# A written issue order, stores on ScalarE's queue and a rewritten 3x3 in a two-layer bottleneck kernel

## The chip, the cores and the metric

The kernel runs on one core of one Trainium2 chip. The metric is the device time of one execution in microseconds (us), as the median of several executions. Their spread is under 0.7% for every kernel. Ratios are computed from the mean time of one kernel's runs over the mean time of the other's in the same rounds on the same chip; they are therefore not quite the ratios of the medians that are quoted beside them. An interval behind a ratio is a 95% interval.

## The reference

Sixteen images of 1024 x 32 x 32 in float32 pass through two residual blocks. The first has a local attention in its middle, the second a 3x3 convolution. Cut to what matters:

```python
def _L0_conv_ref(x, ...):                       # attention block
    residual = x
    h = relu(bn(conv1x1(x, w_conv1)))           # 1024 -> 256
    h = self_att(h, ...)                        # q, k, v: 256 -> 256; 3x3 window, 32 heads of 8, softmax over 9
    h = bn(conv1x1(h, w_conv3))                 # 256 -> 1024
    return relu(h + residual)

def _L1_conv_ref(x, ...):                       # plain block
    out = relu(_bn(_conv(x, w1)))               # 1024 -> 256
    out = relu(_bn(_conv(out, w2, padding=1)))  # 3x3, 256 -> 256
    out = _bn(_conv(out, w3))                   # 256 -> 1024
    return relu(out + x)
```

## The kernel before

TensorE's work for one image is a chain of seven stages: the *attention expansion* (256 -> 1024, tiles `a,w`), the *reduction* of the second block (`r,u`), the *first convolution* of the image two further on (`x,w`), the *3x3* by a Winograd scheme (`v,U`), the *projection* of q, k, v for that later image (`h,wqkv`), its position offsets (`q,pos`), and the *last expansion* (`h,u`). VectorE does the attention of the later image beside these.

An expansion makes its 1024 channels in eight *chunks* of 128. Each chunk has its residual put into PSUM, the memory in which TensorE adds up its products, by ScalarE ahead of the products ("seed" below). ScalarE also evicts the result, and the store follows:

```python
def expand_conv(b, wt, src, shift):
    ahead = []
    def seed(o):
        if o < NC:
            ps = psum.tile([P, HW], F32, tag="ps", name="ps")
            nc.scalar.activation(ps, xr[b, o], AF.Identity)        # residual into PSUM
            ahead.append(ps)
    seed(0)
    seed(1)
    for o in range(NC):
        ps = ahead.pop(0)
        ...                                                        # 8 matmuls onto ps
        nc.scalar.activation(xr[b, o], ps, RELU, bias=shift(o), scale=1.0)
        seed(o + 2)
        yield o

def expand_last(b):
    behind = 2
    for o in expand_conv(b, take("u3", b), hidden_one.pop(b), ...):
        nc.sync.dma_start(out[b, o * P : (o + 1) * P, :], xr.pop((b, o)))   # store
        if o >= behind:
            load_residual(b + 1, o - behind)                                # nc.sync, same buffers
        yield o
    ...
```

The attention works in another layout than the projection writes. So q (`qc<-q`), k (`bnk<-kp`), v (`bnv<-vh`), the offsets (`pc<-po`) and the attention's output (`a<-acc`) are moved by small DMA copies, all issued by SyncE, 36 for an image. The exponential of the softmax is one instruction of ScalarE, between VectorE's logits and VectorE's weighted sum:

```python
        nc.vector.tensor_tensor(e, e, mx..., ALU.subtract)
        nc.scalar.activation(e, e, AF.Exp)
        yield 4.7
```

In this kernel a scheduler chooses the order in which each engine issues; the order of writing is only a wish.

## Time and profile before

| | before |
|---|---|
| median of the three executions before the change was run | 3201.35 us (3199.76 to 3202.84) |
| TensorE busy | 82% of 3198.2 us, mean granted clock 0.908 |
| idle of TensorE before the attention expansion | 442.5 us |
| start to start of that expansion, mean of 13 images | 193.9 us |
| first such start, image 0, image 14 | 216.5, 206.8, 126.6 us |

The last two rows are differences of starts in TensorE's timeline. The kernel has 16 images; 13 of them are alike, the first and the last two are not. So a total is the first start, plus the image 0, plus 13 alike, plus image 14, plus what is left after the start of image 15. The prediction below shows the lines that it rests on.

### The profile page before, as it was taken

How to read it: one execution, taken by the hardware profiler on the slowest of the kernel's cores; microseconds unless marked ns; L12 is line 12 of the kernel's file. 1: busy time of each engine (PE TensorE's matmuls, PEld its weight loads, DVE VectorE, ACT ScalarE, POOL GpSimd, SP SyncE). 2: the span in 40 equal slices, each digit the busy share in tenths (PEclk: the TensorE clock that was granted, in tenths of full speed). 3: DMA queues.
4: the chain of work that ended last, by engine and by line, in shares of the span. 5: the costliest groups of instructions: out<-in, count | busy, mean ns of one | idle time of the engine just before them, and what ended most of it. 6: DMA issues, size and time to landing. Idle time of an engine off the chain costs nothing. (4 is left out here: it accounts for less than half of the span.)

```text
span 3198.2 us, 19613 instructions
## 1 busy us (share of the span) xinstructions
PE 2632.5 (82%) x7072; PEld 1347.0 (42%) x7072; DVE 1959.8 (61%) x1771; ACT 893.6 (28%) x851; POOL 5.0 (0%) x11
## 2 busy tenths in 40 slices
PE   6688579697895969969698796978969699696898
PEld 2335235253352524525244352533525245252545
DVE  2859765855649466485755659566495664757613
ACT  2031322313233132421323223132321324223143
POOL 0000000000000000000000000000000000000000
PEclk9789889798897989989899897989989899798999
DMA  7862726649175491835838276491744828357242
GB/s 226 239 127 76 136 77 166 162 126 198 56 158 151 134 199 60 153 141 151 176 98 179 76 168 160 128 200 58 154 154 141 186 65 169 120 128 173 78 146 92
DMA packets 192783, 446.75 MB, mean 140 GB/s; under 512 B 18096, under 2 KB 124592, under 8 KB 180144
## 3 DMA queue, kind: packets, MB, share of 16 engines
q1 hardware_dynamic: 189696, 434.71, 54.3%
q10 hardware_dynamic: 2992, 10.80, 1.0%
q8 instruction: 57, 0.93, 0.1%
q14 instruction: 38, 0.31, 0.0%
HBM read 285.52 MB, written 73.40 MB: 112 GB/s over the span
## 5 line engine op out<-in xcount | busy, mean ns | idle before, releaser
L289 PE MATMUL ps<-a,w 128*128 128x512 f32 x1024 | 476.3, 628 | 442.5 <-ACT ps L280 442.5
L407 DVE TENSOR_TENSOR prod<-qc,bnk 128x2048 f32<-128x2048 f32 x144 | 323.9, 2287 | 423.4 <-DMA bnk<-kp 252.7
L289 PEld LDWEIGHTS ps<-a,w 128*128 128x128 f32 x1024 | 206.0, 203 | 712.6 <-ACT ps L280 454.7
L260 PE MATMUL ps<-x,w 128*128 128x512 f32 x1024 | 448.7, 598 | 38.2 <-DMA x<-in_x_dram 26.7
L536 PE MATMUL ps<-v,U 128*128 128x256 f32 x2048 | 451.2, 383 | 19.4 <-issue 19.4
L289 PE MATMUL ps<-h,u 128*128 128x512 f32 x1024 | 447.1, 597 | 9.9 <-ACT h L580 9.9
L260 PE MATMUL ps<-r,u 128*128 128x512 f32 x1024 | 442.1, 592 | 0.0
L536 PEld LDWEIGHTS ps<-v,U 128*128 128x128 f32 x2048 | 393.4, 192 | 81.9 <-issue 28.0
L510 DVE TENSOR_TENSOR tv<-vh 128x1088 f32<-128x1088 f32 x64 | 82.4, 1287 | 460.1 <-ACT vh L497 459.5
L340 PE MATMUL ps<-h,wqkv 128*128 128x512 f32 x768 | 339.5, 598 | 3.3 <-ACT kp L350 3.3
L260 PEld LDWEIGHTS ps<-x,w 128*128 128x128 f32 x1024 | 196.3, 192 | 283.9 <-issue 256.4
L289 PEld LDWEIGHTS ps<-h,u 128*128 128x128 f32 x1024 | 195.9, 192 | 257.9 <-issue 245.5
L260 PEld LDWEIGHTS ps<-r,u 128*128 128x128 f32 x1024 | 194.6, 190 | 244.9 <-issue 244.9
L465 DVE TENSOR_TENSOR acc<-acc,term 128x2048 f32<-128x2048 f32 x128 | 291.7, 2279 | 0.6
L453 DVE TENSOR_TENSOR term<-e,bnv 128x2048 f32<-128x2048 f32 x128 | 289.9, 2284 | 0.0
L280 ACT ACTIVATE ps<-r 128x1024 f32<-128x1024 f32 x256 | 257.5, 1021 | 13.8 <-DVE m L558 3.8
L340 PEld LDWEIGHTS ps<-h,wqkv 128*128 128x128 f32 x768 | 145.6, 191 | 188.6 <-issue 179.7
L297 ACT ACTIVATE r<-ps,par 128x1024 f32<-128x1024 f32 x128 | 142.6, 1114 | 244.9 <-PE ps L289 184.8
L515 DVE TENSOR_TENSOR v<-tv 128x512 f32<-128x512 f32 x256 | 160.7, 688 | 75.9 <-DMA a<-acc 68.0
L297 ACT ACTIVATE r<-ps,bn_sh 128x1024 f32<-128x1024 f32 x128 | 142.5, 1113 | 203.4 <-PE ps L289 203.4
L410 DVE TENSOR_TENSOR prod<-prod 128x1024 f32<-128x1024 f32 x144 | 170.3, 1220 | 0.0
L435 ACT ACTIVATE e<-e 128x2304 f32<-128x2304 f32 x16 | 34.0, 2122 | 432.8 <-DVE e L434 432.8
(72 smaller groups left out, 1105.7 us busy)
## 6 DMA issues: line engine op xcount, KB each, us to landing
x<-in_x_dram SPq DMA_DIRECT2D x128, 512.0 KB, 3.7
r<-in_x_dram SPq DMA_DIRECT2D x128, 512.0 KB, 6.2
U<-uw SPq DMA_DIRECT2D x64, 1024.0 KB, 4.9
out_dram<-r SPq DMA_DIRECT2D x128, 512.0 KB, 7.2
bnk<-kp SPq DMA_DIRECT2D x128, 170.0 KB, 10.8
bnv<-vh SPq DMA_DIRECT2D x128, 170.0 KB, 10.2
w<-in_w1t_dram SPq DMA_DIRECT2D x16, 1024.0 KB, 7.1
qc<-q SPq DMA_DIRECT2D x128, 128.0 KB, 5.6
```

The lines of the kernel that those rows point to most:

```text
L260: nc.tensor.matmul(ps[n][:, halves(half)], wt[:, c, n * P : (n + 1) * P], src[:, halves(half)], start=(c == 0), stop=(c == NC - 1),)
L280: nc.scalar.activation(ps, xr[b, o], AF.Identity)
L289: nc.tensor.matmul(ps[:, halves(half)], wt[:, n, o * P : (o + 1) * P], src[:, n, halves(half)], start=False, stop=(n == NW - 1), skip_grou ...
L297: nc.scalar.activation(xr[b, o], ps, RELU, bias=shift(o), scale=1.0)
L340: nc.tensor.matmul(ps[:, halves(half)], wqkv[:, m, at : at + P], h[:, m, halves(half)], start=(m == 0), stop=(m == NW - 1),)
L407: nc.vector.tensor_tensor(by_row(t), by_row(qc), kc[:, :, i : i + JROWS, j : j + W], ALU.mult)
L410: nc.vector.tensor_add(t[:, 0:4], t[:, 0:4], t[:, 4:8])
L453: nc.vector.tensor_tensor(by_row(dst), rows(e[:, k, :]).unsqueeze(1).to_broadcast([P, HEAD_DIM, JROWS, W]), vc[:, :, i : i + JROWS, j : j ...
L465: nc.vector.tensor_add(acc, acc, t)
L510: nc.vector.tensor_tensor(t, vh[:, :, i0 : i0 + 2 * NT - 1 : 2, :], vh[:, :, i1 : i1 + 2 * NT - 1 : 2, :], op)
L515: nc.vector.tensor_tensor(v[:, j].rearrange("p n (r w) -> p n r w", w=NT), t[:, :, :, j0 : j0 + 2 * NT - 1 : 2], t[:, :, :, j1 : j1 + 2 * ...
L536: nc.tensor.matmul(ps[:, at, n * TILES : (n + 1) * TILES], u[:, m, j, n * P : (n + 1) * P], v[:, j, m, :], start=(m == 0 and n == 0), stop ...
```

## The change

Its intent: the order of writing becomes the order of issue on every engine, and the code is written in the order of time. The residual copies for the next expansion come at the end of the last one, so that the exponential can't stand before them; stores go to ScalarE's queue, where the eviction that they wait for has just been issued; k is projected before q; and the 3x3 keeps three of its products in one bank, with ScalarE reading the partial sum on the way, to relieve VectorE. Cut to its core:

```diff
+    ctx.enter_context(tc.manual_schedule())
 ...
+    class Expand:
+        def seed(self):
+            ps = psum.tile([P, HW], F32, tag="ps", name="ps")
+            nc.scalar.activation(ps, xr[self.b, len(self.ahead)], AF.Identity)
+            self.ahead.append(ps)
+        def chunks(self, wt, src, then):
+            for o in range(NC):
+                ...
+                (self.seed if o + 2 < NC else then)()      # `then` seeds the following expansion
+                nc.scalar.activation(xr[self.b, o], ps, RELU, bias=self.shift(o), scale=1.0)
 ...
+        yield from halo("bnk", 1, RELU, kp)                # k, then q, then v and the offsets
+        for n in range(NW):
+            norm(q[:, n, :], conv(0, n), "bnq", n, RELU)
 ...
+        def second(i):                                     # 3x3: on the bank that ScalarE has read
+            products(i, 2, 0, False)
+            both = small("m12")
+            nc.scalar.activation(both, sums[i][:, 0], AF.Identity)
+            diffs[i] = small("d")
+            nc.vector.scalar_tensor_tensor(diffs[i], firsts[i], 2.0, both, ALU.mult, ALU.subtract)
+        def last(i):
+            products(i, 0, 0, False)
+            more_weights()
+            ...                                            # sums on VectorE
             if i + 2 < NU:
                 early.append(next(forms))                  # the transform for product group i + 2
 ...
+        for o in last.chunks(take("u3", b), hidden_one.pop(b), following.seed if following else nothing):
+            nc.scalar.dma_start(out[b, o * P : (o + 1) * P, :], xr.pop((b, o)))
+            if o >= BEHIND:
+                load_residual(b + 1, o - BEHIND)
+            if o == 4 and following:
+                finish_attended(b + 1)
```

The rest of the diff (cut) puts the preparation of the weights beside the first convolution and places the steps of the attention by estimated time.

## The prediction

> **What bounds the kernel now.** I read the page's busy times first, then the groups, the waits, the timeline of one steady image, the granted clock by stretch, and last the waits of the DMA queue.
>
> ```profile
> PE 2632.5 (82%) x7072; PEld 1347.0 (42%) x7072; DVE 1959.8 (61%) x1771; ACT 893.6 (28%) x851; POOL 5.0 (0%) x11
> ...
> L289 PE MATMUL ps<-a,w 128*128 128x512 f32 x1024 | 476.3, 628 | 442.5 <-ACT ps L280 442.5
> L407 DVE TENSOR_TENSOR prod<-qc,bnk 128x2048 f32<-128x2048 f32 x144 | 323.9, 2287 | 423.4 <-DMA bnk<-kp 252.7
> ...
> L260 PE MATMUL ps<-r,u 128*128 128x512 f32 x1024 | 442.1, 592 | 0.0
> ```
>
> TensorE (PE) is the busiest engine, and of its 566 us of idle time 442.5 us stand before one line: the expansion of the attention block (L289, a,w), which waits for ScalarE's copy of the residual into PSUM (L280). The same matmuls elsewhere (L260, r,u) wait for nothing. The timeline of one image shows why:
>
> ```profile
> 1354.77 8.32 PE L289 MATMUL ps<-h,u 128*128 128x512 f32 x19
> 1394.04 29.13 PE L289 MATMUL ps<-a,w 128*128 128x512 f32 x64 [30.95 <-ACT ps L280]
> 1423.01 27.63 PE L260 MATMUL ps<-r,u 128*128 128x512 f32 x64
> 1450.47 27.63 PE L260 MATMUL ps<-x,w 128*128 128x512 f32 x64
> 1477.94 27.79 PE L536 MATMUL ps<-v,U 128*128 128x256 f32 x128
> 1505.57 13.90 PE L340 MATMUL ps<-h,wqkv 128*128 128x512 f32 x32
> ```
>
> ```profile
> 1363.18 1.11 ACT L297 ACTIVATE r<-ps,bn_sh 128x1024 f32<-128x1024 f32 x1 [2.38 <-PE ps L289]
> 1390.95 2.12 ACT L435 ACTIVATE e<-e 128x2304 f32<-128x2304 f32 x1 [26.65 <-DVE e L434]
> 1392.98 2.90 ACT L280 ACTIVATE ps<-r 128x1024 f32<-128x1024 f32 x3
> ```
>
> (Columns: start, us, engine, work, idle before it and releaser.) ScalarE stands 26.65 us at the exponential of the next image but one, because VectorE is still computing its logits; the residual copies that TensorE needs are queued behind it. Nothing real joins the two. TensorE loses 31 us per image so. The start of L289 (a,w) goes from 423.37 to 2943.65 in 13 images: 193.9 us each.
>
> **What the Trainium skill says.** (1) "Perfetto Trace Analysis", Per-engine timelines: ScalarE and VectorE are strict first-in-first-out. The trace agrees: the copies above start 0.1 us before the exponential's row ends, never ahead of it. (2) "TensorE: Matmul & The Clock Gate", HAM oscillation: an idle gap above some 3.4 us drops the array to half clock, regained after some microseconds of work. The trace agrees: the first block after each gap takes 29.1 to 30.8 us, the same block without a gap 27.63, and the granted clock is 1.00 from 1423 to 1556 us but 0.58 from 1556 to 1586. So a gap costs about 2.5 us more. (3) "DMA: Bandwidth & Descriptors", Issuing engines are not separate DMA queues: issue from another engine saves sequencer time only, all use the same 16 DMA engines. The trace of before has only start-up copies on ScalarE's queue.
>
> **The change, part by part.** The work of one steady image on TensorE, from the spacing of starts: four blocks of 27.47, the 3x3 27.63, q, k, v and the offsets 13.83 + 1.87 + 6.97: 160.2 us. Matmul counts stay. That is the floor.
>
> *Written order, residual copies before the eviction.* The first two copies for the next expansion now come at chunks 6 and 7 of the last one; the exponential is written after some 18 steps of 3.0 us, thus behind the attention expansion's last eviction. VectorE's logits take 9 x 4.3 + 12 = 51 us in the trace (interleaved); written in order, dependent instructions follow each other at 0.46 us where independent ones take 0.34 (rows of 0.42 us), so I take 9 x 4.75 + 9 = 52. They end some 62 us after the expansion begins, the exponential's turn comes at about 57 to 68. ScalarE hardly waits and TensorE does not: -30.9 and -2.7 us (clock) per image.
>
> *Sums of the 3x3.* Products of four matmuls take 27.63/16 = 1.73 us. Each second product accumulates on a bank that ScalarE must first have copied (0.60 us), with one product between: hidden. VectorE drops from 16 x 0.685 + 4 x 1.22 = 15.8 to 16 x 0.685 = 11.0 us, ScalarE gains 6 x 0.6. But the fourth transform now stands behind two additions that wait for ScalarE's copy of the second sum: 15.5 (products end) + 0.9 + 1.4 + 1.3 + 1.3 = 20.4 us after the 3x3 begins, needed at 19.0. **+1.5 us.**
>
> *k first, stores on ScalarE's queue.* Here I expect a new wait. The DMA queue's own waits in one image:
>
> ```profile
> SPq L390 <- DMA bnk<-kp: 4.0, 4, 1.1
> SPq L369 <- DMA bnk<-kp: 3.9, 4, 1.0
> SPq L595 <- DMA bnv<-vh: 3.4, 3, 1.2
> ```
>
> The stores (L595) do not read bnv, yet wait for it. In the trace's DMA rows the completion semaphores are eight, taken in turn, and each issue waits for the transfer eight before; at start-up the two queues share the same eight. So a store on ScalarE will wait for a copy issued by SyncE, and ScalarE with it, since nothing passes a waiting issue. In the new order, from the start of the projection (p): k 8 copies, q 4, a 8, q 4, v 4, offsets 4, v 4, one weight, then store 0, whose eighth predecessor is the second offsets copy. The DMA engines are full there (share 1.04 and 1.11 from 1512 to 1556 us). In before 28 such copies land in 37 us; I split it as 1.5 us for k and v, 1.0 for q and a, 1.25 for offsets. Up to that copy: 8 x 1.5 + 8 + 8 + 4 x 1.5 + 2.5 = 36.5 us, from p + 5: p + 41. The expansion begins at p + 22.7, so store 0 is held to 18.5 us into it, not 4.9. Copies for chunks 0 to 2 are made before it; chunk 3 (due at 10.3) starts at 18.5 + 0.4 + 1.0 = 20: **+9.7 us, and 2 us of clock.** The later stores follow at the pace of the copies, 1.5 us apart, ahead of TensorE.
>
> Steady image: 160.2 + 1.5 + 11.7 = 173.4; 13 images: 2254 us.
>
> *The ends.* Start-up: the weights' preparation is put beside and behind the first convolution (it ends at 40.6), which then keeps the projection's evictions until about 64 us; the exponential of image 0 is written after the third convolution (about 147 us), and its weighted sum of 44 us, copies and evictions follow: the first expansion at about 208 us (216.5 before). Image 0 has no convolution beside it, so image 1's attention still has 40 us to do in the projection, and copies and stores wait for it: 190 us (206.8 before). Image 14: 25 us of attention are put before the stores: 144 (126.6). Image 15: 124 (123). Tail 5.
>
> Sum: 208 + 190 + 2254 + 144 + 124 + 5 = **2925 us** with the store wait.
>
> **Rivals.** *A: the stores don't hold ScalarE* (other semaphores, or the copies land sooner). Then a steady image is 161.9 us, image 0 some 178, image 14 some 133: 2753 us. For it: the change chooses this queue on purpose, and k first moves its copies some 7 us earlier. Against: the three lines above. *B: the wait for the exponential only moves,* with VectorE too late for the new place. 101 us of attention in order, 15 of transforms and 11 of sums are 127 us of 160, and its present idle 28 us after the projection shrinks; against it. If VectorE came 10 us late per image: 130 us more, about 3050. *C: VectorE in order bounds the 3x3:* if the third transform is late too, some 4 us more per image, 50 us.
>
> **Range and chances.** I give the store wait 65%, A 35%: 0.65 x 2925 + 0.35 x 2753 = 2865; I put 2870. The range takes A's sum less 15 as its low end, 2740, and the store wait with C, 2970, as its high end. Faster by over 2% means under 3137, which only B and more would miss: 0.98.
>
> **What would show it.** Right: the wait of L289 (a,w) for L280 falls from 442.5 us to under 60; the 3x3 shows a gap of 1 to 2 us before its 12th product; the expansion after the 3x3 shows one gap of 7 to 12 us before its fourth chunk, at L280, while ScalarE's queue waits for the offsets copies (pc). If that gap is missing A holds. Wrong: ScalarE idle for VectorE at the exponential with TensorE idle beside it (B), or many gaps in the 3x3 (C). The prediction fails if the semaphores' order is not the written one, or if a pool's buffers are handed out so that VectorE waits for TensorE.

## The result

The changed kernel takes **3235.62 us** (median of 4, 3234.0 to 3246.05) against 3200.96 us for the kernel before in the same rounds (the three executions of the table above and a fourth): ratio 1.0115 [1.0093, 1.0136], the same within 2%, and far outside the predicted range of 2740 to 2970 us.

The groups of the page of the changed kernel (line, engine, tiles, count; busy us and mean ns; idle before and its releaser):

```profile
PE 2678.3 (83%) x7048; PEld 1349.6 (42%) x7048; DVE 1945.8 (60%) x1693; ACT 951.4 (29%) x947; POOL 5.1 (0%) x11
...
L298 PE MATMUL ps<-a,w 128*128 128x512 f32 x1024 | 475.6, 627 | 293.4 <-ACT ps L289 255.1
L421 DVE TENSOR_TENSOR prod<-qc,bnk 128x2048 f32<-128x2048 f32 x144 | 329.0, 2285 | 646.9 <-DMA qc<-q 646.8
L298 PE MATMUL ps<-h,u 128*128 128x512 f32 x1024 | 479.1, 629 | 142.2 <-ACT ps L289 135.7
```

TensorE's idle time before the attention expansion has fallen (442.5 to 293.4 us), but a second idle place has opened in the middle of the last expansion (`h,u`: 142.2 us), and VectorE waits 646.8 us for the copies of q. The timeline of TensorE over one image (start, us, work, idle before it):

```profile
1390.31 29.40 PE L298 MATMUL ps<-a,w 128*128 128x512 f32 x64 [18.46 <-ACT ps L289]
...
1477.06 17.68 PE L558 MATMUL ps<-v,U 128*128 128x256 f32 x80 [0.69 <-ACT m L572]
1496.63 5.42 PE L558 MATMUL ps<-v,U 128*128 128x256 f32 x24 [1.89 <-issue]
1502.80 3.72 PE L558 MATMUL ps<-v,U 128*128 128x256 f32 x16 [0.75 <-ACT m L580]
1506.35 17.33 PE L349 MATMUL ps<-h,wqkv 128*128 128x512 f32 x40
...
1561.19 5.26 PE L298 MATMUL ps<-h,u 128*128 128x512 f32 x8 [7.98 <-ACT ps L289]
1586.11 30.48 PE L298 MATMUL ps<-a,w 128*128 128x512 f32 x64 [19.66 <-ACT ps L289]
```

From 1390.31 to 1586.11 are 195.8 us, which is also the mean of the 13 images. The gaps add up to 0.69 + 1.89 + 0.75 + 7.98 + 19.66 = 31.0 us; with the 160.2 us of work and the slower blocks after the gaps (29.40 us where a block with no gap before it takes 27.63) that is the whole. So the floor is what the prediction said, and the question is what makes the gaps of 8 and 20 us. ScalarE in the same image:

```profile
1420.81 2.11 ACT L451 ACTIVATE e<-e 128x2304 f32<-128x2304 f32 x1
...
1533.80 0.34 ACTq L702 DMA_DIRECT2D out_dram<-r  x1
...
1550.89 1.24 ACT L493 ACTIVATE a<-a,par 128x1024 f32<-128x1024 f32 x1 [3.39 <-DMA a<-acc]
1558.99 1.24 ACT L493 ACTIVATE a<-a,par 128x1024 f32<-128x1024 f32 x1 [6.86 <-DMA a<-acc]
...
1585.03 1.03 ACT L289 ACTIVATE ps<-r 128x1024 f32<-128x1024 f32 x1 [22.86 <-DMA r<-in_x_dram]
```

The exponential (L451) no longer has an idle time before it. The first store goes out 1.1 us after its eviction began, so it isn't held. But ScalarE stands 3.39 and 6.86 us at the activation of the attention output, because its copies (`a<-acc`) are late, and 22.86 us at a residual, because its load is late. Both are issued by SyncE, whose issues run like this:

```profile
1519.80 20.65 SPq L384 DMA_DIRECT2D qc<-q  x4
1540.54 13.80 SPq L487 DMA_DIRECT2D a<-acc  x8
1554.45 3.60 SPq L384 DMA_DIRECT2D qc<-q  x4
...
1561.49 10.14 SPq L403 DMA_DIRECT2D pc<-po  x4
...
1583.78 2.08 SPq L90 DMA_DIRECT2D r<-in_x_dram  x2
```

Four copies of q took 20.65 us to *issue*. The waits of SyncE's queue name what they waited for (total us, times, longest):

```profile
SPq L384 <- DMA out_dram<-r: 211.7, 16, 15.1
...
SPq L487 <- DMA out_dram<-r: 114.5, 39, 4.7
SPq L403 <- DMA out_dram<-r: 97.5, 13, 8.2
```

The copies of q (L384), of the attention output (L487) and of the offsets (L403) wait for *stores*, which touch none of their data. A *completion semaphore* is a counter that tells when a transfer has landed. The DMA records of the trace give the semaphore of each transfer, and from them I listed its previous user (start of the issue, queue, transfer, semaphore, previous user and its start; rows left out):

```
1519.80 Sync   qc<-q        sem 108   bnk<-kp      1513.11
1522.95 Sync   qc<-q        sem 100   bnk<-kp      1515.25
1524.49 Sync   qc<-q        sem 102   bnk<-kp      1515.89
1533.80 Scalar out_dram<-r  sem 101   u<-ws        1500.35
1537.23 Scalar out_dram<-r  sem 105   bnk<-kp      1511.23
1539.90 Sync   qc<-q        sem 105   out_dram<-r  1537.23
1540.66 Scalar out_dram<-r  sem 107   bnk<-kp      1512.47
1543.92 Sync   a<-acc       sem 107   out_dram<-r  1540.66
1546.85 Sync   a<-acc       sem 109   out_dram<-r  1544.10
1552.48 Sync   a<-acc       sem 101   out_dram<-r  1547.53
1562.20 Scalar out_dram<-r  sem 108   a<-acc       1544.55
1569.78 Sync   pc<-po       sem 108   out_dram<-r  1562.20
```

There are eight semaphores for the two queues, and an issue waits until the previous transfer on its semaphore has landed. That much the prediction had. But the third and the fourth copy of q are 15.4 us apart, because semaphore 105 had been dealt to the second store first. In the order of writing that store stands some 25 transfers later. The semaphores were dealt out in an order other than the written one, with the stores ahead. Over the whole run, 297 of the 1123 transfers of the two queues, taken in the order in which they were issued, don't have the next of the eight semaphores in turn; in the kernel before it is 29, and with the stores back on SyncE (st_sync below) 19. So SyncE waits for ScalarE, not ScalarE for SyncE. The rest follows: the attention output lands late, ScalarE stands at its activation, the seed and the next stores stand behind that; the copy of the offsets then waits for the store at 1562.20; and the residual loads, the last in SyncE's line, come so late that ScalarE waits 22.86 us for one.

### The profile page after: what moved, and what is told of

Same layout as the page of the kernel before. It is cut to its first block, busy times and chain, and to the rows that moved or that the text cites. A ratio compares the mean times of both kernels' runs of the same rounds, so it can differ in the third digit from the quotient of the medians.

```text
span 3233.4 us, 19507 instructions
## 1 busy us (share of the span) xinstructions
PE 2678.3 (83%) x7048; PEld 1349.6 (42%) x7048; DVE 1945.8 (60%) x1693; ACT 951.4 (29%) x947; POOL 5.1 (0%) x11
## 4 chain that ended last, share of the span: by engine, by line
PE 73%; DMA 13%; DVE 4%; ACT 3%; SPq 3%; issue 2%; ACTq 0%; DVEq 0%
PE ps L267 26%; PE ps L298 23%; PE ps L558 15%; PE ps L349 9%; DMA out_dram<-r 5%; DMA r<-in_x_dram 5%; DMA a<-acc 2%; DVE acc L481 1%; DVE term L469 1%; SPq L372 1%; SPq L487 1%; ACT r L307 1%; ACT ps L289 1%; PE ps L392 1%; SPq L403 1%
## 5 line engine op out<-in xcount | busy, mean ns | idle before, releaser
L298 PE MATMUL ps<-a,w 128*128 128x512 f32 x1024 | 475.6, 627 | 293.4 <-ACT ps L289 255.1
L421 DVE TENSOR_TENSOR prod<-qc,bnk 128x2048 f32<-128x2048 f32 x144 | 329.0, 2285 | 646.9 <-DMA qc<-q 646.8
L298 PE MATMUL ps<-h,u 128*128 128x512 f32 x1024 | 479.1, 629 | 142.2 <-ACT ps L289 135.7
L558 PE MATMUL ps<-v,U 128*128 128x256 f32 x2048 | 474.2, 390 | 65.3 <-issue 42.3
L298 PEld LDWEIGHTS ps<-h,u 128*128 128x128 f32 x1024 | 205.6, 203 | 411.9 <-issue 239.5
L267 PEld LDWEIGHTS ps<-x,w 128*128 128x128 f32 x1024 | 195.8, 191 | 280.1 <-issue 253.9
L349 PEld LDWEIGHTS ps<-h,wqkv 128*128 128x128 f32 x768 | 145.1, 191 | 184.1 <-issue 171.2
L522 DVE TENSOR_TENSOR tv<-vh 128x1088 f32<-128x1088 f32 x64 | 82.3, 1286 | 166.3 <-ACT vh L510 166.2
L321 ACT ACTIVATE h<-ps,par 128x1024 f32<-128x1024 f32 x32 | 38.5, 1205 | 403.8 <-PE ps L267 403.2
```

The costliest lines, as they stand in the source:

```text
L267: nc.tensor.matmul(ps[n][:, halves(half)], wt[:, c, n * P : (n + 1) * P], src[:, halves(half)], start=(c == 0), stop=(c == NC - 1),)
L298: nc.tensor.matmul(ps[:, halves(half)], wt[:, n, o * P : (o + 1) * P], src[:, n, halves(half)], start=False, stop=(n == NW - 1), skip_grou ...
L349: nc.tensor.matmul(ps[:, halves(half)], wqkv[:, m, at : at + P], h[:, m, halves(half)], start=(m == 0), stop=(m == NW - 1),)
L421: nc.vector.tensor_tensor(by_row(t), by_row(qc), kc[:, :, i : i + JROWS, j : j + W], ALU.mult)
L522: nc.vector.tensor_tensor(t, vh[:, :, i0 : i0 + 2 * NT - 1 : 2, :], vh[:, :, i1 : i1 + 2 * NT - 1 : 2, :], op)
L558: nc.tensor.matmul(sums[i][:, at, n * TILES : (n + 1) * TILES], u[:, m, j, n * P : (n + 1) * P], v[:, j, m, :], start=(start and m == 0 an ...
```

## The experiments

Each was run three rounds beside the kernel before, and each gave a correct result. Theory 1 is the one just told: the two queues share their completion semaphores, and SyncE's copies wait for stores. Theory 2: the DMA engines are simply full after the projection, and it doesn't matter who issues. Theory 3 (the prediction's rivals B and C): VectorE in the written order comes too late.

### Stores on GpSimd's queue (st_pool)

```diff
-            nc.scalar.dma_start(out[b, o * P : (o + 1) * P, :], xr.pop((b, o)))
+            nc.gpsimd.dma_start(out[b, o * P : (o + 1) * P, :], xr.pop((b, o)))
```

> The changed kernel with its stores issued from GpSimd's queue, whose completion semaphores are not those of the other two queues; all else, bytes included, is the same. Theory 1 (shared ring of eight semaphores: SyncE's copies of q and of the attended rows wait for stores that ScalarE issues later): the first four q copies take under 5 us instead of 20.6, the residual copies stop waiting for late loads, the gaps of 8 and 19 us before the last chunk and the next expansion go, a steady image takes 162 to 170 us instead of 195, in all 2720 to 2850 us. Theory 2 (the copies in this order are simply too much for the DMA engines): no change, 3200 to 3260 us.

Measured: **2952.5 us**, ratio 0.9232 [0.9216, 0.9248]. SyncE's issues in this run:

```profile
1413.11 2.72 SPq L384 DMA_DIRECT2D qc<-q  x4
1416.41 9.68 SPq L487 DMA_DIRECT2D a<-acc  x8
...
1442.45 5.20 SPq L90 DMA_DIRECT2D r<-in_x_dram  x4
...
1453.00 16.58 SPq L90 DMA_DIRECT2D r<-in_x_dram  x4
```

The four copies of q now issue in 2.72 us instead of 20.65, for the same bytes through the same DMA engines: theory 2 falls, theory 1 holds. Theory 3 falls with it as the cause of the loss: VectorE runs the same instructions in the same order as in the changed kernel, and 283 us are gone. (In the trace the transfers of GpSimd's queue use eight semaphores of their own, 111 to 118; those of the two other queues are within 100 to 109.) An image takes 174.3 us in the mean. The time missed the expected 2720 to 2850, because a gap before the attention expansion stays (6.3 us in the image shown): the residual loads are issued by SyncE behind all its copies.

### Stores on SyncE's queue, as before (st_sync)

```diff
-            nc.scalar.dma_start(out[b, o * P : (o + 1) * P, :], xr.pop((b, o)))
+            nc.sync.dma_start(out[b, o * P : (o + 1) * P, :], xr.pop((b, o)))
```

> The changed kernel with its stores issued from SyncE's queue, as before the change. Theory 1 (shared ring): one queue, so a copy can only wait for what was issued before it; ScalarE never issues. The copies come 20 us earlier, but the stores then stand behind them and the residual loads behind the stores' landing, so a gap of some 8 us before the next expansion is left: 172 to 178 us per image, 2850 to 2960 us in all. Theory 2 (DMA engines full): 3200 to 3260 us.

Measured: **2977.57 us**, ratio 0.9309 [0.9279, 0.9339], just above the expected span, with a gap of 5.4 to 7.8 us before the attention expansion in the three images that I looked at. Within one queue the issues have one order, with the stores behind the copies, and the copies of q wait for no store. So the one word `scalar` costs 3235.6 - 2977.6 = 258 us in the changed kernel.

### The changed kernel without the written order (no_order)

```diff
-    ctx.enter_context(tc.manual_schedule())
```

> The changed kernel without the written order: the scheduler may reorder each engine's instructions as it did in the kernel before. If the written order is what removed the 31 us wait behind the exponential, that wait comes back: L298 (a,w) waits 300 us or more for ScalarE in all and the time is 3050 to 3250 us. If the order of the calls (copies before the eviction) is what removed it, the wait stays away and the time falls under 2950 us.

Measured: **3369.85 us**, ratio 1.0538 [1.0522, 1.0553], slower than either expectation. TensorE's idle time before the attention expansion is 632.5 us. The waits of this run (all engines, then SyncE's queue) show both costs side by side, the old one of the exponential and the new one of the copies of q for stores:

```profile
ACT e L451 <- DVE e L448: 438.3, 16, 62.5
```

```profile
SPq L384 <- DMA out_dram<-r: 343.2, 69, 14.0
```

### The kernel before, with its stores on ScalarE's queue (before_st_act)

```diff
-            nc.sync.dma_start(out[b, o * P : (o + 1) * P, :], xr.pop((b, o)))
+            nc.scalar.dma_start(out[b, o * P : (o + 1) * P, :], xr.pop((b, o)))
```

> The kernel before with one part of the change alone: stores issued from ScalarE's queue. Theory 1 (shared ring) says that the two queues then hold each other up here too: SyncE's copies wait for stores or ScalarE's residual copies stand behind held stores, 3200 to 3300 us, with waits of SyncE's queue for stores other than those of the residual loads. Theory 2: 3190 to 3210 us, as before.

Measured: **3342.75 us**, ratio 1.0453 [1.0438, 1.0469], above the expected 3200 to 3300 us. The coupling needs nothing else of the change. In the kernel before no copy of q, k or v waits for a store; here those of k (L369) do:

```profile
SPq L369 <- DMA out_dram<-r: 354.9, 56, 18.6
```

### The kernel before, in the written order (before_order)

```diff
     nc = tc.nc
+    ctx.enter_context(tc.manual_schedule())
```

> The kernel before with nothing changed but that each engine issues in the written order. If the wait of ScalarE at the exponential comes from the scheduler's order alone, as the prediction's first step has it, that wait (26.7 us per image) and most of TensorE's 31 us go, and the time is 2850 to 3050 us even without the rewriting of the rest. If the order of writing had to be arranged by time first, TensorE finds other waits and the time is 3150 us or more.

Measured: **2960.72 us**, ratio 0.9253 [0.9237, 0.927]. One line takes 238 us off (3198.3 us for the kernel before in these rounds). The wait of ScalarE at the exponential falls from 432.8 to 46.4 us in all; a group of the page and one image of ScalarE's timeline:

```profile
L290 PE MATMUL ps<-a,w 128*128 128x512 f32 x1024 | 475.6, 628 | 80.8 <-ACT ps L281 80.8
```

```profile
1503.88 2.12 ACT L436 ACTIVATE e<-e 128x2304 f32<-128x2304 f32 x1 [2.72 <-DVE e L435]
```

The idle time before the attention expansion falls from 442.5 to 80.8 us, and an image from 193.9 to 171.2 us. The first step of the prediction is shown by this run, apart from everything else.

### The same, and the stores on ScalarE's queue (before_order_act)

```diff
-            nc.sync.dma_start(out[b, o * P : (o + 1) * P, :], xr.pop((b, o)))
+            nc.scalar.dma_start(out[b, o * P : (o + 1) * P, :], xr.pop((b, o)))
```

> The kernel before in the written order (which took 2961 us with its stores on SyncE), and its stores on ScalarE's queue; nothing else of the change. Theory 1 (shared ring): SyncE's copies of q, k, v wait for stores that ScalarE has not issued yet, also with q first and the old 3x3, at some 10 to 18 us per image: 3100 to 3250 us. Rival (only k first, or the new writing by time, makes the stores collide): within 1% of 2961 us.

Measured: **3236.29 us**, ratio 1.0124 [1.0109, 1.0139], that is 276 us more than the run above. It is also the time of the whole change, with 0.7 us between them: the written order and the queue of the stores alone already give that time. That the two agree so closely is chance: here the 13 images that are alike take 191.2 us each against 195.8, and the first start, image 0 and image 14 together 619 us (244.0 + 221.6 + 153.2) against 556 (225.2 + 187.8 + 143.0).

```profile
SPq L370 <- DMA out_dram<-r: 400.7, 56, 17.0
```

### Stores and residual loads on GpSimd's queue (st_pool_r)

```diff
-            nc.sync.dma_start(t, x[b, c * P : (c + 1) * P, :])       # in load_residual
+            nc.gpsimd.dma_start(t, x[b, c * P : (c + 1) * P, :])
```

on top of st_pool.

> The changed kernel with its stores and its residual loads both on GpSimd's queue. Theory 1 (the ring of eight completion semaphores that SyncE's and ScalarE's queues share is the cause; what is left in the run with the stores alone on GpSimd is the late residual loads, which SyncE issues behind the copies): the gap of 5 to 6 us before the attention expansion and the 2.5 us of clock behind it go, 173.9 us per image becomes 165 to 167, and the time 2830 to 2870 us. Rival: those residual loads are late because the stores land late (same buffer), whoever issues them: then the time stays within 1% of 2952 us.

Measured: **2845.06 us**, ratio 0.8898 [0.8885, 0.8912], inside the expected span. An image takes 167.1 us. So the late residual loads cost st_pool 7 us of the 14 by which its image stood above the floor of 160.2; they were late because of their place in SyncE's line, not because the stores landed late.

### The same, and the transforms before the sums (st_pool_rw)

```diff
         def last(i):
             products(i, 0, 0, False)
             more_weights()
+            if i + 2 < NU:
+                early.append(next(forms))
             ...                                   # sums on VectorE
-            if i + 2 < NU:
-                early.append(next(forms))
```

> The run before, and in the 3x3 the third and fourth transforms are written before the VectorE additions of the same step. If the prediction's step on the 3x3 is right (the fourth transform stands behind two additions that wait for ScalarE's copy of the second sum), the gap of 1.9 us before the 12th product goes: 16 x 1.9 = 30 us less than the run before, 2800 to 2840 us. If the gap only moves (a bank of the sums now freed later), the time is within 0.3% of the run before.

Measured: **2798.84 us**, ratio 0.8741 [0.872, 0.8763]: 46 us less than the run before, where 30 were worked out. The gap of 1.89 us before the 12th product is gone, and the group's idle time falls; first st_pool_r, then st_pool_rw:

```profile
L558 PE MATMUL ps<-v,U 128*128 128x256 f32 x2048 | 481.7, 395 | 65.5 <-issue 42.3 <-ACT m L580 12.2 <-ACT m L572 11.0
```

```profile
L558 PE MATMUL ps<-v,U 128*128 128x256 f32 x2048 | 464.1, 387 | 35.3 <-ACT m L580 12.2 <-issue 12.1 <-ACT m L572 11.0
```

The idle time falls by 30.2 us, as worked out, and the same matmuls are 17.6 us less busy: a gap within the 3x3 also slows the products near it.

### The 3x3 as before (st_pool_r_old33)

The function of the 3x3 is put back as it was; stores and residual loads are on GpSimd's queue, all else is as in the changed kernel.

```diff
-        def first(i): ...
-        def third(i): ...
-        def second(i): ...
-        def last(i): ...
+        for i in range(NU):
+            u, v = take(f"U{i}", b), early.pop(0)
+            inner = products(u, v, (1, 2))
+            ...                                   # as in the kernel before
```

> The changed kernel with stores and residual loads on GpSimd's queue (2845 us), and the 3x3 as it was before. If the new 3x3 costs TensorE 3.3 us per image and VectorE has room for the older sums (it idles some 25 us per image for the copies), 16 x 3.3 = 53 us and some clock go: 2780 to 2800 us. If VectorE's 4.8 us more per image, or a buffer of the old sums, end up on the path, the time is 2845 us or more.

Measured: **2764.73 us**, ratio 0.8643 [0.8625, 0.8662], the fastest of all, 80 us less than st_pool_r and below the expected 2780 to 2800. The page's busy times, and its group of the 3x3:

```profile
PE 2604.9 (94%) x7048; PEld 1330.4 (48%) x7048; DVE 2018.7 (73%) x1757; ACT 881.9 (32%) x851; POOL 141.4 (5%) x267
...
L549 PE MATMUL ps<-v,U 128*128 128x256 f32 x2048 | 450.8, 383 | 12.1 <-issue 12.1
```

VectorE is busy longer than in the changed kernel (2018.7 against 1945.8 us) and TensorE doesn't notice. An image takes 161.9 us, 1.7 us above the floor of 160.2. Relieving VectorE brought nothing, as VectorE did not set the pace.

### q first again (st_pool_r_qfirst)

```diff
-        yield from halo("bnk", 1, RELU, kp)
         q = ppool.tile([P, NW, HW], F32, tag="t", name=f"q_{b}")
         ...
             yield "q", n
+        yield from halo("bnk", 1, RELU, kp)
```

(with the two steps that hang on the first and the fourth product moved along), on top of st_pool_r.

> The changed kernel with stores and residual loads on GpSimd's queue (2845 us), and q projected first again. The first product of the logits needs both q and k; it starts 34.2 us after the projection in that run, 31.0 in the kernel before with q first. If k first gains nothing, the time stays within 0.7% of 2845 us; if k first brings the logits forward, it is 2880 us or more.

Measured: **2836.71 us**, ratio 0.8875 [0.8861, 0.889]. That is 8 us (0.3%) less than with k first; the intervals overlap. k first gains nothing.

### The copies on GpSimd's queue, the stores left on ScalarE's (copies_pool)

```diff
-                    nc.sync.dma_start(by_head(t, n, j), ...)         # k, v; likewise q, pc and a
+                    nc.gpsimd.dma_start(by_head(t, n, j), ...)
```

> The changed kernel with its stores left on ScalarE's queue, and the copies of q, k, v, the offsets and the attention output moved to GpSimd's queue. Theory 1 (shared ring): the copies no longer wait for stores, VectorE no longer idles some 49 us per image for q, and the time falls as in the run with the stores on GpSimd, to 2880 to 2990 us. Rival (ScalarE itself is slowed by issuing stores, or the stores collide with the copies on the DMA engines): the time stays above 3150 us.

Measured: **3045.36 us**, ratio 0.9524 [0.9509, 0.954]. This is a miss: below the rival's 3150, but 55 us above the span of theory 1. Part of it holds. No copy waits for a store any more, VectorE's first logits start 36.3 us after the projection has begun instead of 57.6, and ScalarE issues the stores as in the changed kernel, so that its issuing them is not the cost. But a new wait came in, on VectorE in the weighted sum, and TensorE's 3x3 behind it (the two timelines of this run):

```profile
1400.00 2.29 DVE L469 TENSOR_TENSOR term<-e,bnv 128x2048 f32<-128x2048 f32 x1 [17.07 <-PE ps L558]
```

```profile
1410.48 12.25 PE L558 MATMUL ps<-v,U 128*128 128x256 f32 x48 [10.53 <-ACT m L572]
```

The instructions of VectorE are the same, in the same order, as in st_pool. But in the trace 28 of the attention's instructions wait for TensorE where st_pool has 16; the twelve more are all a `term`. In the code `term` and the transforms take turns in the four buffers of one pool; so I infer that here a `term` got a buffer that holds a transform until the 3x3 has read it. Twelve images have this wait (220.9 us in all on VectorE). The 10.5 us, and some 2 us for the clock after it, are about what lies between 181.4 us per image here and the 167 to 174 us of the two runs with the stores on GpSimd. That this wait accounts for the whole excess was not tested by itself.

### The kernel before in the written order, stores and residual loads on GpSimd's queue (before_order_pool)

```diff
+    ctx.enter_context(tc.manual_schedule())
-            nc.sync.dma_start(t, x[b, c * P : (c + 1) * P, :])       # in load_residual
+            nc.gpsimd.dma_start(t, x[b, c * P : (c + 1) * P, :])
-            nc.sync.dma_start(out[b, o * P : (o + 1) * P, :], xr.pop((b, o)))
+            nc.gpsimd.dma_start(out[b, o * P : (o + 1) * P, :], xr.pop((b, o)))
```

> The kernel before in the written order with its stores and residual loads on GpSimd's queue; q first, old 3x3, old ends. If the written order and the separate queue are what is to be had, the gaps of 2.2 and 3.8 us and their 2 us of clock go from 170 us per image, 162 to 165 are left, and the time is 2810 to 2870 us, no longer than the changed kernel with the same queues (2845 us). If writing the rest by time, k first and the sums read on the way are worth something of their own, it stays above 2890 us.

Measured: **2939.72 us**, ratio 0.92 [0.9184, 0.9215]. Of the two expectations the second came true, above 2890: writing the rest by time is worth something of its own, 2939.7 - 2845.1 = 95 us against st_pool_r. The table says where: mostly not in the 13 images that are alike (168.5 against 167.1 us, 13 x 1.4 = 18 us), but at the ends (253.9 + 201.2 + 157.3 = 612 against 223.4 + 176.0 + 142.4 = 542, 70 us). But st_pool_r carries the new 3x3. The closer pair is st_pool_r_old33, with the old 3x3 in both: 2939.7 - 2764.7 = 175 us, of which 13 x 6.6 = 86 lie in the images that are alike and 81 at the ends (612 against 531).

### All runs together

First start, image 0, mean of 13 and image 14 are spacings of the attention expansion in each run's timeline of TensorE.

| kernel | issue order | stores | median us | ratio | first start | image 0 | mean of 13 | image 14 |
|---|---|---|---|---|---|---|---|---|
| before | scheduler | SyncE | 3201.0 | 1 | 216.5 | 206.8 | 193.9 | 126.6 |
| before_st_act | scheduler | ScalarE | 3342.8 | 1.0453 | 216.4 | 187.6 | 204.6 | 150.1 |
| before_order | written | SyncE | 2960.7 | 0.9253 | 243.9 | 205.5 | 171.2 | 153.0 |
| before_order_act | written | ScalarE | 3236.3 | 1.0124 | 244.0 | 221.6 | 191.2 | 153.2 |
| before_order_pool | written | GpSimd, with residuals | 2939.7 | 0.9200 | 253.9 | 201.2 | 168.5 | 157.3 |
| the change | written | ScalarE | 3235.6 | 1.0115 | 225.2 | 187.8 | 195.8 | 143.0 |
| no_order | scheduler | ScalarE | 3369.9 | 1.0538 | 201.1 | 198.3 | 206.5 | 155.1 |
| copies_pool | written | ScalarE, copies GpSimd | 3045.4 | 0.9524 | 229.2 | 178.4 | 181.4 | 140.8 |
| st_sync | written | SyncE | 2977.6 | 0.9309 | 227.5 | 191.4 | 175.8 | 144.8 |
| st_pool | written | GpSimd | 2952.5 | 0.9232 | 226.2 | 188.8 | 174.3 | 141.4 |
| st_pool_r | written | GpSimd, with residuals | 2845.1 | 0.8898 | 223.4 | 176.0 | 167.1 | 142.4 |
| st_pool_r_qfirst | written | as above, q first | 2836.7 | 0.8875 | 221.8 | 176.2 | 166.2 | 143.5 |
| st_pool_rw | written | as above, k first, transforms first | 2798.8 | 0.8741 | 224.2 | 172.7 | 163.6 | 142.9 |
| st_pool_r_old33 | written | as above, old 3x3 | 2764.7 | 0.8643 | 223.6 | 169.6 | 161.9 | 137.8 |

## Why the prediction was wrong

**What bounds the kernel: right.** That the wait before the attention expansion is an order of issue on ScalarE and nothing real is shown by before_order: one line, and 238 us go.

**Written order, -30.9 and -2.7 us per image: right in kind, and mostly in size.** In the changed kernel the exponential waits for nothing. In before_order the image gets 22.7 us shorter; the rest of the 33.6 is taken by two gaps of 2.2 and 3.8 us, the clock after them, and what else that kernel's order costs.

**Sums of the 3x3, +1.5 us: too small.** The gap before the 12th product came as worked out (1.89 us for 1.5). But "with one product between: hidden" failed in two places of sixteen, where the product for the other half of the PSUM tile is written directly behind the first or the second one: it waits for ScalarE's copy of the neighbouring half (0.69 and 0.75 us). The gaps are 3.3 us per image. Undoing the new 3x3 was worth 80 us in all: 5.2 us in each of the 13 images alike (167.1 - 161.9), of which 3.3 are the gaps and 1.9 the slower matmuls beside them (481.7 against 450.8 us busy over 16 images).

**k first, stores on ScalarE's queue, +11.7 us: this is the step that failed.** Its words are "So a store on ScalarE will wait for a copy issued by SyncE, and ScalarE with it". That took the ring of eight to be dealt out in the written order. It is not: semaphores were dealt to stores ahead of copies that are written and issued before them. The wait goes the other way: not +11.7 us in one gap before the fourth chunk, but 8.0 us before the eighth chunk and 19.7 us before the next attention expansion, each with a slower clock after it. The table of semaphores shows the direction; before_st_act (+143 us), before_order_act (+276 us) and st_sync (-258 us) show the size, in three settings. Against the prediction's sum the miss in the images alike is 13 x (195.8 - 173.4) = 291 us of the 311 us between its 2925 and the measured 3235.6 us. Both mechanisms need the same fact, that an issue waits for an older transfer without any tie of data, and three lines of the profile had shown it. For the direction, who stands before whom, the kernel before held a sign that the prediction didn't use. At start-up, where its two queues share the semaphores, SyncE's copies of k (L369) wait for transfers that ScalarE issued and that they don't read (the weights of the 3x3, uw):

```profile
SPq L369 <- DMA uw<-u: 16.9, 3, 14.1
```

The prediction put 65% on one answer and left the other out.

**The ends.** Predicted 208, 190, 144 and 129 us; measured 225.2, 187.8, 143.0 and 131.7 (3233.4 less the last start, 3101.7). Three of four numbers were right, one of them for a reason that didn't hold: without a hold of the stores, rival A put image 14 at 133, yet it takes 142.4 in st_pool_r, so the 144 is not owed to the store wait. The start-up was 17 us too short; it is 222 to 226 us also where stores don't touch the copies, and 201.1 us for the same code without the written order (no_order). So it is the order in which the start-up is written, not the stores; which part of it was not followed further.

**Rivals and range.** Rival A, no hold, was put at 161.9 us per image (its own terms, 160.2 + 1.5, give 161.7) and 2753 us in all. The run nearest to that case is st_pool_r, the changed kernel with no store or residual load on the shared semaphores: 167.1 us and 2845.1. That st_pool_r_old33 has 161.9 and 2764.7 is in part luck: A's figure holds 1.5 us for the new 3x3, which that run doesn't have. What the run does show is that the floor was well worked out: 1.7 us are left above it. Rivals B and C did not happen in the changed kernel. The range was too narrow because all its cases let SyncE run freely: it held the wait that I had worked out and its absence, but not the same wait in the other direction. The prediction's last sentence ("fails if the semaphores' order is not the written one") named the very condition and gave it no weight.

**The clock after a gap, 2 to 2.5 us: right in size.** In the changed kernel a block of the attention expansion takes 29.40 and 30.48 us behind its gap, against 27.63. But the 3.4 us of the prediction's second point are no threshold in these traces. In before_order 14 gaps of 2.2 us before the last expansion were followed by a block of 29.3 to 29.4 us in eight images and of 27.73 us in six, and one gap of 3.79 us before the attention expansion by a block of 27.73. In the changed kernel the 24 products behind the gap of 1.89 us took 5.42 us in 13 images and 7.11 in three.

**What stays open.** Why the semaphores are dealt in that order was not found; the runs only show that they are, when two queues share them. No kernel with the stores on ScalarE and the semaphores in the written order was run, so the size that I predicted for that case was never measured. And st_pool's 174.3 us per image comes close to the predicted 173.4 for another reason (late residual loads), which is no confirmation.

## What to carry to other kernels

Before a DMA is moved to another engine's queue, find out which transfers share a completion semaphore with it, and read the queue's own waits after the change: a copy that waits for a store it has nothing to do with is the sign, and a queue with semaphores of its own (here GpSimd's) was the cure in this kernel. A written order is worth much where the scheduler puts a long wait ahead of urgent work, but it should be tried by itself: here one line gave 238 us, and one of the parts that came with it, the queue of the stores, took more than that back. And relieving an engine that doesn't set the pace brings nothing, and may cost the one that does.

## What the Trainium skill lacked or had wrong

- "DMA: Bandwidth & Descriptors", Issuing engines are not separate DMA queues: it says that issuing from several engines only saves the sequencer's time. That leaves out the completion semaphores. Moving the stores from SyncE to ScalarE cost 276 us of 2961 (before_order_act), moving them from ScalarE to GpSimd gained 283 us of 3236 (st_pool), with the same bytes on the same DMA engines; the issue itself takes 0.34 us on ScalarE and 0.53 us on GpSimd in the traces.
- "DMA: Bandwidth & Descriptors", Why a DMA increments its semaphore by 16 and not by 1: it asks for one semaphore per in-flight slot, which agrees with what the traces show. It doesn't say that slots may be few and shared: in these programs eight serve two queues, so that a copy of q stood 15.4 us until a store had landed which is written behind it.
- "PSUM — Partial Sum Buffer", The four PSUM rules: it allows a synchronised read of a partial sum in the middle of an accumulation group; the results with the new 3x3 are correct, which agrees. It doesn't tell the price: a product that follows directly waited 0.69 to 0.75 us for the copy, although it writes the other half of the tile. Whether that wait is needed, or only kept by the program, was not tested.
- No page that I used has it that moving DMAs to another queue can change the waits between two other engines: the same VectorE instructions in the same order had twelve more waits for TensorE, up to 19.2 us each (copies_pool). That buffers of a pool were dealt out otherwise is inferred.
